# A recommender's forward pass on one core: token rows summed in fours, one comparison a step, one transposed feature buffer, and evictions a step later

## The chip, the cores and the metric

The kernel runs on one core of a Trainium2 chip. The metric is device time in microseconds of one execution, and lower is better. A core has five engines with queues of their own: TensorE (PE, with its weight loads as PEld), VectorE (DVE), ScalarE (ACT), GpSimd (POOL) and SyncE (SP). An engine works through its queue in order. Data comes from HBM by DMA into SBUF, and TensorE writes its results to PSUM.

## The reference

There are 16,384 samples. Each has 32 word indices into a table of 50,000 x 300, three lists of 20 indices into small tables (1000, 5000 and 10000 rows of 64), and four single indices into tables of 100, 50, 20 and 1000 rows of 64. Each small table has a second table of width 1, the "wide" one.

```python
tok = word_emb[token_idx].mean(axis=1)                  # 300 wide
e1 = emb_mh1[mh1_idx].mean(axis=1)                      # e1, e2, e3: 64 wide each
...
o1 = emb_oh1[oh1_idx]                                   # o1 to o4: 64 wide each
...
emb = jnp.concatenate([tok, e1, e2, e3, o1, o2, o3, o4], axis=1)   # 748 wide
wide = (wide_mh1[mh1_idx].sum(axis=(1, 2)) + ... + wide_oh4[oh4_idx][:, 0])
h = relu(emb @ W1 + b1); h = relu(h @ W2 + b2); h = relu(h @ W3 + b3)   # 1024, 512, 256
return sigmoid(h @ Wd + bd + wide)
```

## The kernel before

**Tiles and steps.** The samples are worked through in 128 tiles of 128. A tile takes 11 steps (`STEPS`); a step handles six of the 64 pairs of samples in a tile (`ONEHOT`), and the last step four. The main loop writes all engines' instructions out step by step under a manual schedule, so the order in each engine's queue is the order in which the loop emits them. After the last tile 16 more steps follow (`WAKE`).

**Small tables.** They aren't gathered. Per step `one_hots` compares each key with a row of numbers (`iota`, kept in the PSUM tile `own`) and so makes one-hot rows: `row1` (index modulo 128) and `slice1` (index divided by 128, counted through all 138 slices of all small tables), each with an instruction of its own (L326). ACT scales the upper half of `row1` (L333), so that two samples share one column. `counts` (L344) multiplies the two on TensorE, and ACT packs the result into `cnt` as bytes (L347): how often each row of each table occurs in each sample. One tile later `small_sums` (L363) multiplies `cnt` by the tables, which stand in SBUF as three bf16 terms (`terms`, made at the start by `convert_tables` at a pace set by `TABLE_PACE`), into one PSUM tile `pg` per pair of tables; DVE adds up the three terms into the features `g` (L369).

**Tokens.** The word rows are gathered from HBM by POOL, one indirect DMA for each of the 32 indices of a tile (L259), 128 rows of 300 numbers each, two DMAs to one buffer of `tok_rows`. There are six such buffers. `add_up` adds the two rows to the running sum `tok_sum`, which is in PSUM, with one addition a row (L241, L243, L247), three pairs behind the gathers in the program (`TOK_LAG`). The gathers and additions are spread evenly over all steps.

**Transposes and MLP.** Two steps after a tile's sums are there, `add_small` and `add_tokens` transpose its features on TensorE (four and three transposes, L405, L408, L424, L425), each into a PSUM tile, and DVE copies them with the factors of the means into `x_small`, `x_tok` and `wide_row` (L409 to L427). Three tiles make a block (the last two tiles are blocks of one). Once a block is complete, `mlp` runs on TensorE (L462, f32, up to 384 columns), cut into pieces that are spread over the steps until the next block should be ready. ACT applies bias and ReLU right behind the last matmul of each output (L471).

In a step the loop emits: the one-hots of the next step, `counts` of this one, the table conversion at the start, transposes, gathers and additions, `small_sums` with the reduction behind each pair, then its share of the MLP. At the end, `early_part` begins the last block's first layer with the chunks that need no tokens.

```python
counts(cnt, hot_now, i)
...
if waiting and step >= waiting[0][0]:
    block = transpose(*waiting.pop(0)[1:])
...
toks.to(n_all * (step + 1) / n_steps)
...
    done = next(sums)
...
    layers.to(mlp_work * layers.size * (step + 1 - begin) / left + ahead)
```

Of the kernel before, what the change touches and what calls it, by code (L numbers as in the profile page):

```python
# [23 lines left out]
TOK_GROUP = 2  # L24
TOK_LAG = 3
TOK_BUFS = 6
WAKE = 16
EARLY = 3
BLOCK = 512
# [10 lines left out]
TABLE_PACE = 1.3  # L40
# [5 lines left out]
SMALL = ("o4", "e1", "e2", "e3", "o1", "o2", "o3")  # L46
WIDE_IN_FRONT = ("mh1", "mh3", "oh2")
G_COLS = 7 * ROW
# [7 lines left out]
def kernel(  # L56
# [27 lines left out]
    tables = {"o4": oh4, "e1": mh1, "e2": mh2, "e3": mh3, "o1": oh1, "o2": oh2, "o3": oh3}  # L84
    slices, n_h = {}, 0
    for f in SMALL:
# [9 lines left out]
    ohp = ctx.enter_context(tc.tile_pool(name="onehot", bufs=2))  # L96
# [3 lines left out]
    xsp = ctx.enter_context(tc.tile_pool(name="x_small", bufs=2))  # L100
    xtp = ctx.enter_context(tc.tile_pool(name="x_tok", bufs=2))
# [7 lines left out]

    chunk_rows = [  # L110
        [(300, 428)],
        [(428, 556)],
        [(556, 684)],
        [(684, 748), (256, 300)],
        [(0, 128)],
        [(128, 256)],
    ]
    chunk_k = [sum(b - a for a, b in rows) for rows in chunk_rows]
    NK = len(chunk_rows)

# [4 lines left out]
    scale = const.tile([P, 3], F32, name="scale")  # L125
# [3 lines left out]

# [4 lines left out]
    tok_sum = own[:, 128 : 128 + TOK_D]  # L134
# [13 lines left out]


# [61 lines left out]

# [9 lines left out]
    def load_weights():  # L221
        for k, rows in enumerate(chunk_rows):
            at = 0
            for a, b in rows:
                nc.sync.dma_start(out=w1_sb[at : at + b - a, k, :], in_=w1[a:b, :])
                at += b - a
        nc.sync.dma_start(out=w2_sb, in_=w2.rearrange("(k p) m -> p k m", p=P))
        nc.sync.dma_start(out=w3_sb, in_=w3.rearrange("(k p) m -> p k m", p=P))
        for sb, dram in ((wd_sb, wd), (b1_sb, b1), (b2_sb, b2), (b3_sb, b3), (bd_sb, bd)):
            nc.sync.dma_start(out=sb, in_=dram)  # L230

    n_groups = N_TOK // TOK_GROUP
    n_all = B // P * n_groups + TOK_LAG
    sums_of = {}
    token_indices = {}

    def add_up(t, q, rows):

        a, b = rows[:, 0:TOK_D], rows[:, TOK_D : 2 * TOK_D]
        if q == 0:  # L240
            nc.vector.tensor_add(tok_sum, a, b)  # L241
        else:
            nc.vector.tensor_add(tok_sum, tok_sum, a)  # L243
            to = tok_sum
            if q == n_groups - 1:
                to = sums_of[t] = gp.tile([P, TOK_D], F32, name="g_tok")
            nc.vector.tensor_add(to, tok_sum, b)  # L247

    def tokens():

        under_way = []
        for n in range(n_all):
            if n < n_all - TOK_LAG:
                t, q = divmod(n, n_groups)
                it = token_indices[t // NSUB][:, t % NSUB, :].bitcast(U32)
                rows = tokp.tile([P, TOK_GROUP * TOK_D], F32, name="tok_rows")
                for r in range(TOK_GROUP):
                    j = q * TOK_GROUP + r
                    nc.gpsimd.indirect_dma_start(  # L259
                        out=rows[:, r * TOK_D : (r + 1) * TOK_D],  # L260
                        out_offset=None,
                        in_=word,
                        in_offset=bass.IndirectOffsetOnAxis(ap=it[:, j : j + 1], axis=0),
                    )
                under_way.append((t, q, rows))
            if n >= TOK_LAG:
                add_up(*under_way.pop(0))
            yield 1

    def load_indices(blk):  # L270
# [7 lines left out]
        ix = keyp.tile([P, NSUB // 2, 2, N_SMALL], I32, name="ix")  # L278
        for s in range(NSUB):
            nc.sync.dma_start(  # L280
                out=ix[(s % 2) * HALF : (s % 2 + 1) * HALF, s // 2],
# [7 lines left out]
    def lookup_keys(ix):  # L289

        pairs = NSUB // 2
        low = keyp.tile([P, pairs, 2, N_SMALL], I32, name="low", tag="low")
        nc.vector.tensor_single_scalar(low, ix, P - 1, op=ALU.bitwise_and)
        nc.vector.tensor_single_scalar(ix, ix, 7, op=ALU.logical_shift_right)
        keys = keyp.tile([P, pairs, 2, 2 * N_SMALL], BF16, name="keys", tag="keys")
        for r in range(pairs):
            view = keys[:, r].rearrange("p w (f c) -> p w f c", f=2)
            nc.vector.tensor_copy(view[:, 0], low[:, r])
            nc.vector.tensor_add(view[:, 1], ix[:, r], first)
        return keys  # L300

    def key_columns(keys):


        pairs = NSUB // 2
        pk = ps_h.tile([P, pairs, 2, P], BF16, name="pk", tag="ph")
        for r in range(pairs):
            for w in range(2):
                nc.tensor.transpose(pk[:, r, w, :], keys[:, r, w, :], ident_bf)
        sc = scp.tile([P, pairs, 2, 2, HALF, 2], BF16, name="sc")  # L310
        n = pairs * 2 * P
        nc.vector.tensor_copy(
            sc.rearrange("p r w t b d -> p (r w t b) d"),
            pk.rearrange("p r w b -> p (r w b)").unsqueeze(2).to_broadcast([P, n, 2]),
        )
        return sc

    def one_hots(sc, s, i):
# [3 lines left out]
        row1 = ohp.tile([P, ONEHOT, P], BF16, name="row1")  # L322
        slice1 = ohp.tile([P, ONEHOT, n_h], BF16, name="slice1")
        for w, (one, n) in enumerate(((row1, P), (slice1, n_h))):
            shape = [P, rows, n // 2, 2]
            nc.vector.tensor_tensor(  # L326
                one[:, 0:rows, :].rearrange("p i (n d) -> p i n d", d=2),
                iota[:, 0:n].rearrange("p (n d) -> p n d", d=2).unsqueeze(1).to_broadcast(shape),
                sc[:, s // 2, w, s % 2, b : b + rows, :].unsqueeze(2).to_broadcast(shape),
                ALU.is_equal,  # L330
            )
        upper = row1[HALF:P, 0:rows, :]
        nc.scalar.activation(upper, upper, AF.Copy, scale=UPPER)  # L333
        return row1, slice1

    def counts(cnt, hot, i):
# [5 lines left out]
        for k in range(rows):  # L342
            at = k % n * n_h
            nc.tensor.matmul(  # L344
                pc[:, k // n, at : at + n_h], hot[0][:, k, :], hot[1][:, k, :], start=True, stop=True
# [7 lines left out]
    def small_sums(g, cnt):  # L353
# [3 lines left out]
        for i in (0, 2, 4, 6):  # L357
            pair = SMALL[i : i + 2]
            pg = ps_g.tile([P, 2, 3 * ROW], F32, name="pg")
            for j, f in enumerate(pair):  # L360
                h0, h1 = slices[f]
                for h in range(h0, h1):
# [3 lines left out]
                    yield 1  # L366
            at = i * ROW
            n = len(pair)
            nc.vector.tensor_reduce(  # L369
                g[:, at : at + n * ROW].rearrange("p (f d) -> p f d", f=n),  # L370
                pg[:, 0:n, :].rearrange("p f (c d) -> p f d c", c=3),
                AX.X,
                ALU.add,
            )
            yield None

    def wide_term(g):
# [4 lines left out]
            g[:, EMB : EMB + 6 * ROW].rearrange("p (c d) -> p c d", d=2 * ROW)[:, :, 0:2],  # L382
# [3 lines left out]
        nc.vector.tensor_add(g[:, EMB : EMB + 1], wide, g[:, G_COLS - 1 : G_COLS])  # L386

    class Block:
# [3 lines left out]
        def __init__(self, first, n):  # L392
            self.first, self.n, self.missing = first, n * P, 2 * n
            self.small = xsp.tile([P, 4, N], F32, name="x_small")
            self.wide = wp.tile([1, N], F32, name="wide_row")
            self.tok = None

        def columns(self, t):
            return slice((t - self.first) * P, (t - self.first + 1) * P)

        def add_small(self, t, g):

            at = self.columns(t)
            pt = ps_h.tile([P, 4, P], F32, name="pt", tag="ph")
            nc.tensor.transpose(pt[:, 3, :], g[:, 0:P], ident)  # L405
            for k in range(3):
                c = (1 + 2 * k) * ROW + 1
                nc.tensor.transpose(pt[:, k, :], g[:, c : c + P], ident)  # L408
            nc.vector.tensor_tensor(  # L409
                self.small[:, 0:3, at], pt[:, 0:3, :], scale.unsqueeze(2).to_broadcast([P, 3, P]), ALU.mult  # L410
            )
            nc.vector.tensor_copy(self.small[0:EMB, 3, at], pt[0:EMB, 3, :])  # L412
            nc.vector.tensor_copy(self.wide[:, at], pt[EMB : EMB + 1, 3, :])  # L413

        def add_tokens(self, t, g):


            if self.tok is None:
                self.tok = xtp.tile([P, 2, N], F32, name="x_tok")
            at = self.columns(t)  # L420
            rest = TOK_D - 2 * P
            pt = ps_h.tile([P, 3, P], F32, name="pt", tag="ph")
            for k in range(2):
                nc.tensor.transpose(pt[:, k, :], g[:, k * P : (k + 1) * P], ident)  # L424
            nc.tensor.transpose(pt[0 : EMB + rest, 2, :], g[:, TOK_D - rest - EMB : TOK_D], ident)  # L425
            nc.vector.tensor_single_scalar(self.tok[:, :, at], pt[:, 0:2, :], 1.0 / N_TOK, op=ALU.mult)  # L426
            nc.vector.tensor_single_scalar(  # L427
                self.small[EMB : EMB + rest, 3, at], pt[EMB : EMB + rest, 2, :], 1.0 / N_TOK, op=ALU.mult
            )

        def chunk(self, k):
            x = self.small[:, k, :] if k < 4 else self.tok[:, k - 4, :]
            return x[: chunk_k[k], 0 : self.n]

    def early_part(block):
# [3 lines left out]
        for pair in range(2):  # L439
            two = ps_c.tile([P, 2, 512], F32, name="pc")  # L440
            for m in range(2):
                part.append(two[:, m, :])
                for k in range(NK - 3):
# [8 lines left out]

    def layer(dst, weights, bias, srcs, n_out, part=None):

# [210 lines left out]
```

## Time and profile before

| what | value |
|---|---|
| median of 10 runs | 5192.75 us (5188.0 to 5193.59) |
| the profiled execution | 5189.72 us, its span from the first to the last instruction 5187.9 us |
| PE, PEld busy | 4843.9 us (93%), 3552.2 us (68%) |
| DVE, ACT busy | 3856.3 us (74%), 2758.4 us (53%) |
| POOL busy | 3876.6 us (75%), 4096 gathers of 946 ns |
| DMA | 652 MB, 126 GB/s on average |
| mean granted TensorE clock | 0.983 |

Busy time is the time in which an engine had an instruction under way, by kind of instruction. It doesn't count the time that a queue spends between two instructions, and the ends of pipelined matmuls are modelled. Idle time is put down to what ended it; "issue" is idle time that ends with nothing that the profile shows. A line such as L259 is a line of the listing above.

### The profile page before, as it was taken

To read this page: it belongs to the slowest core of one execution; us is meant where nothing else is said; L and a number is where in the kernel's file an instruction comes from. 1 tells how busy PE (TensorE), PEld (TensorE's weight loads), DVE (VectorE), ACT (ScalarE), POOL (GpSimd) and SP (SyncE) were. 2 spreads that over 40 slices of the span, in tenths; PEclk is the share of its full clock that TensorE was granted. 3 is DMA by queue.
4 is the path that set the end of the run, shared out by engine and by line. 5 is a ranking of instruction groups with operands and counts; after the bars stand their busy time and mean duration, and the time that the engine had idled before them with its cause. 6 is when DMAs were issued, how large, how long until landed. Compare 5 with 4: busy or idle time off the path is not lost.

```text
span 5187.9 us, 94821 instructions
## 1 busy us (share of the span) xinstructions
PE 4843.9 (93%) x34940; PEld 3552.2 (68%) x34940; DVE 3856.3 (74%) x8481; ACT 2758.4 (53%) x3538; POOL 3876.6 (75%) x4103
## 2 busy tenths in 40 slices
PE   7899999999999999999999999999999999999999
PEld 4676676767667766666776667666666666676667
DVE  7777777777777777777777777777777777777773
ACT  6555555555555555555555555555555555555552
POOL 7777777777777777777777777777777777777774
PEclk9999999999999999999999999999999999999999
DMA  7444444444444444444444444444444444444442
GB/s 197 124 126 126 124 127 126 124 125 126 126 124 126 126 126 124 127 126 124 125 126 126 124 126 126 125 124 128 125 123 126 125 126 124 125 126 126 124 124 72
DMA packets 252899, 652.00 MB, mean 126 GB/s; under 512 B 119035, under 2 KB 119591, under 8 KB 252435
## 3 DMA queue, kind: packets, MB, share of 16 engines
q0 software_dynamic: 196608, 629.41, 44.2%
q1 hardware_dynamic: 55827, 16.53, 1.4%
q8 instruction: 276, 4.52, 0.3%
q14 instruction: 188, 1.54, 0.1%
HBM read 645.59 MB, written 0.07 MB: 124 GB/s over the span
## 4 chain that ended last, share of the span: by engine, by line
PE 30%; DMA 24%; DVE 17%; issue 17%; POOL 11%; ACT 1%; DVEq 0%; SPq 0%; POOLq 0%; ACTq 0%
DMA tok_rows<-in_word_emb_dram,it 23%; PE ph L462 17%; POOL tok_rows L259 11%; PE pg L363 9%; DVE own L247 6%; DVE own L243 3%; DVE slice L326 3%; PE pc L344 3%; DVE row L326 2%; PE po L487 1%; DVE g L369 1%; DVE wide_row L413 0%; DVE x_small L427 0%; DMA w_sb<-in_W_dram 0%; DVE x_small L412 0%
## 5 line engine op out<-in xcount | busy, mean ns | idle before, releaser
L259 POOL DMA_INDIRECT tok_rows<-in_word_emb_dram,it x4096 | 3875.8, 946 | 1278.3 <-issue 773.4
L333 ACT ACTIVATE row<-row 64x768 bf16<-64x768 bf16 (+1 forms) x1408 | 1155.4, 821 | 1577.3 <-DVE row L326 1556.0
L363 PE MATMUL pg<-terms,cnt 128*128 128x195 bf16 x17664 | 1760.6, 248 | 223.0 <-DVE g L369 221.8
L363 PEld LDWEIGHTS <-cnt 128*128 128x128 fp8e3 x17664 | 1526.4, 98 | 178.2 <-issue 172.1
L347 ACT ACTIVATE cnt<-pc 128x828 uint16<-128x828 f32 (+1 forms) x1408 | 1191.7, 846 | 157.3 <-PE pc L344 123.0
L462 PE MATMUL ph<-h,w_sb 128*128 128x384 f32 (+1 forms) x3520 | 1260.5, 497 | 0.5 <-ACT h L471 0.5
L247 DVE TENSOR_TENSOR own<-own,tok_rows 128x300 f32<-128x300 f32 x1792 | 857.3, 478 | 468.8 <-DMA tok_rows<-in_word_emb_dram,it 425.7
L243 DVE TENSOR_TENSOR own<-own,tok_rows 128x300 f32<-128x300 f32 x1920 | 918.4, 478 | 265.8 <-DMA tok_rows<-in_word_emb_dram,it 209.8
L462 PE MATMUL ph<-x_small,w_sb 128*128 128x384 f32 (+1 forms) x2784 | 1009.8, 486 | 6.1 <-DVE x_small L409 3.3
L344 PEld LDWEIGHTS <-row 128*128 128x128 bf16 x8192 | 599.7, 98 | 591.4 <-issue 284.5
L462 PEld LDWEIGHTS ph<-h,w_sb 128*128 128x128 f32 x3520 | 636.7, 198 | 388.1 <-issue 110.9
L326 DVE TENSOR_TENSOR row<-own,sc 128x768 bf16<-128x768 bf16 (+1 forms) x1408 | 761.7, 541 | 129.1 <-PE pc L344 29.8
L326 DVE TENSOR_TENSOR slice<-own,sc 128x828 bf16<-128x828 bf16 (+1 forms) x1408 | 795.1, 565 | 0.0
L344 PE MATMUL pc<-slice,row 128*128 128x138 bf16 x8192 | 740.9, 225 | 54.7 <-ACT row L333 53.5
L471 ACT ACTIVATE h<-ph,b_sb 128x384 f32<-128x384 f32 (+1 forms) x612 | 350.0, 572 | 624.4 <-PE ph L462 599.8
L462 PEld LDWEIGHTS ph<-x_small,w_sb 128*128 128x128 f32 x2784 | 484.4, 191 | 246.0 <-issue 20.7
L462 PE MATMUL ph<-x_tok,w_sb 128*128 128x384 f32 (+1 forms) x1392 | 530.3, 485 | 0.0
L369 DVE TENSOR_REDUCE g<-pg 128x130 f32<-128x390 f32 (+1 forms) x512 | 258.4, 505 | 101.2 <-PE pg L363 99.9
L462 PEld LDWEIGHTS ph<-x_tok,w_sb 128*128 128x128 f32 x1392 | 242.0, 191 | 112.6 <-issue 5.2
L241 DVE TENSOR_TENSOR own<-tok_rows 128x300 f32<-128x300 f32 x128 | 61.3, 479 | 110.2 <-DMA tok_rows<-in_word_emb_dram,it 109.1
L426 DVE TENSOR_SCALAR x_tok<-pt 128x256 f32<-128x256 f32 x128 | 53.7, 419 | 107.1 <-PE pt L425 106.6
L409 DVE TENSOR_TENSOR x_small<-pt,scale 128x384 f32<-128x384 f32 x128 | 70.2, 548 | 35.8 <-PE pt L408 34.8
(56 smaller groups left out, 873.8 us busy)
## 6 DMA issues: line engine op xcount, KB each, us to landing
tok_rows<-in_word_emb_dram,it POOLq DMA_INDIRECT x4096
ix<-in_idx_dram SPq DMA_DIRECT2D x128, 32.0 KB
w_sb<-in_W_dram SPq DMA_DIRECT2D x6, 512.0 KB
raw<-in_mh_dram SPq DMA_DIRECT2D x4, 682.5 KB
it<-in_idx_dram SPq DMA_DIRECT2D x32, 64.0 KB
w_sb<-in_W_dram SPq DMA_DIRECT2D x1, 2048.0 KB
out_dram<-h SPq DMA_DIRECT2D x42, 1.5 KB
raw<-in_mh_dram SPq DMA_DIRECT2D x2, 227.5 KB
```

What stands on the lines that cost most here:

```text
L243: nc.vector.tensor_add(tok_sum, tok_sum, a)
L247: nc.vector.tensor_add(to, tok_sum, b)
L259: nc.gpsimd.indirect_dma_start(out=rows[:, r * TOK_D : (r + 1) * TOK_D], out_offset=None, in_=word, in_offset=bass.IndirectOffsetOnAxis(ap ...
L326: nc.vector.tensor_tensor(one[:, 0:rows, :].rearrange("p i (n d) -> p i n d", d=2), iota[:, 0:n].rearrange("p (n d) -> p n d", d=2).unsque ...
L333: nc.scalar.activation(upper, upper, AF.Copy, scale=UPPER)
L344: nc.tensor.matmul(pc[:, k // n, at : at + n_h], hot[0][:, k, :], hot[1][:, k, :], start=True, stop=True)
L347: nc.scalar.activation(cnt[:, :, b : b + rows].rearrange("l h (g k) -> l h g k", g=2), pc[:, :, 0 : n * n_h].rearrange("l g (k h) -> l h g ...
L363: nc.tensor.matmul(pg[:, j, :], by_slice[:, h, :], terms[:, h, :], start=(h == h0), stop=(h == h1 - 1))
L369: nc.vector.tensor_reduce(g[:, at : at + n * ROW].rearrange("p (f d) -> p f d", f=n), pg[:, 0:n, :].rearrange("p f (c d) -> p f d c", c=3) ...
L409: nc.vector.tensor_tensor(self.small[:, 0:3, at], pt[:, 0:3, :], scale.unsqueeze(2).to_broadcast([P, 3, P]), ALU.mult)
L462: nc.tensor.matmul(ph[:, 0:n], weights[: src.shape[0], k, m * P : (m + 1) * P], src, start=(k == 0), stop=(k == len(srcs) - 1),)
L471: nc.scalar.activation(dst[:, m, 0:n], ph[:, 0:n], AF.Relu, bias=bias[:, m : m + 1])
```

## The change

- **Tokens.** A buffer of `tok_rows` now has five rows: four gathered ones (`TOK_GROUP = 4`) and, in front, the sum so far. One `tensor_reduce` adds up the five and writes the result into the front row of the next group's buffer, for the last group into the features. There are three such buffers. The gathers are the same and still emitted two at a time, and the reduction of a group follows when it is three pairs behind.
- **One-hots.** Both one-hots of a sample lie side by side in one tile `hot`, and one comparison over 138 columns makes them; there are three such tiles instead of two.
- **Features.** The small sums and the token sum stand in one buffer `g`, with the columns in an order in which six transposes of 128 columns take in everything, the wide term too (column `WIDE_AT`, with a zero row in `W1`). They go into one PSUM tile of two banks, and one `tensor_tensor` with a factor for each chunk copies all into `x`.
- **Evictions.** What reads TensorE's results is emitted later: the reductions of `pg` and the copies of the transposes at the end of the step (`later`, `flush`) or at the end of the next one, ACT's ReLU ahead of the last matmul of the next output or at the next step's start (`pending`, `flush_outputs`). `small_sums` runs by a fixed table of steps, and most of its matmuls come right behind `counts`.
- **Rest.** Indices are loaded and keys prepared for blocks of two tiles instead of four, `TABLE_PACE` is 1.5 for 1.3, and the order of two tables is swapped.

```diff
-TOK_GROUP = 2
+TOK_PAIR = 2
+TOK_GROUP = 4
 TOK_LAG = 3
-TOK_BUFS = 6
+TOK_BUFS = 3
+HOT_BUFS = 3
-BLOCK = 512
+BLOCK = 256
-TABLE_PACE = 1.3
+TABLE_PACE = 1.5
...
-        a, b = rows[:, 0:TOK_D], rows[:, TOK_D : 2 * TOK_D]
-        if q == 0:
-            nc.vector.tensor_add(tok_sum, a, b)
+        begin = 1 if q == 0 else 0
+        if q == N_TOK // TOK_GROUP - 1:
+            to = features(t)[:, TOK_AT:G_COLS]
+            summed.add(t)
         else:
-            nc.vector.tensor_add(tok_sum, tok_sum, a)
-            to = tok_sum
-            if q == n_groups - 1:
-                to = sums_of[t] = gp.tile([P, TOK_D], F32, name="g_tok")
-            nc.vector.tensor_add(to, tok_sum, b)
+            to = after[:, 0, :]
+        nc.vector.tensor_reduce(to, rows[:, begin:, :].rearrange("p r d -> p d r"), AX.X, ALU.add)
...
-        for w, (one, n) in enumerate(((row1, P), (slice1, n_h))):
-            shape = [P, rows, n // 2, 2]
-            nc.vector.tensor_tensor(
...
+        hot = ohp.tile([P, 2 * ONEHOT, n_h], BF16, name="hot")
+        shape = [P, 2 * rows, n_h // 2, 2]
+        nc.vector.tensor_tensor(
+            hot[:, 0 : 2 * rows, :].rearrange("p i (n d) -> p i n d", d=2),
+            iota.rearrange("p (n d) -> p n d", d=2).unsqueeze(1).to_broadcast(shape),
+            sc[:, at : at + rows].rearrange("p b w d -> p (b w) d").unsqueeze(2).to_broadcast(shape),
+            ALU.is_equal,
+        )
...
+        def transpose(self, t, ks):
...
+            for j, k in enumerate(ks):
+                c = chunk_at[k]
+                nc.tensor.transpose(pt[:, j // n, j % n, :], g[:, c : c + P], ident)
+            def evict():
+                nc.vector.tensor_tensor(
+                    self.x[:, ks[0] : ks[-1] + 1, at : at + P].rearrange("p (a c) b -> p a c b", a=banks),
+                    pt,
...
+    early_sums = {1: sizes_of_pairs[0], 9: sizes_of_pairs[2], **{i: large for i in range(3, 8)}}
+    late_sums = {2: large, 10: sizes_of_pairs[3]}
...
+            flush_outputs()
             counts(cnt, hot_now, i)
             tables_on_chip.to(TABLE_PACE * (step - 2))
...
+        if sums:
+            run_sums(sums, early_sums.get(i, 0), step, step)
         if waiting and step >= waiting[0][0]:
...
         if layers:
             layers.to(mlp_work * layers.size * (step + 1 - begin) / left + ahead)
+        if sums:
+            run_sums(sums, late_sums.get(i, 0), step, step + 1)
+        flush(step)
```

## The prediction

> **What bounds the kernel now.** I read the page's first table, then the costliest groups, then what POOL waited for, then the POOL rows of the timeline, and last the busy time by stretches.
>
> From the page, engines and groups (busy, mean of one, idle before):
>
> ```profile
> PE 4843.9 (93%) x34940; PEld 3552.2 (68%) x34940; DVE 3856.3 (74%) x8481; ACT 2758.4 (53%) x3538; POOL 3876.6 (75%) x4103
> ...
> L259 POOL DMA_INDIRECT tok_rows<-in_word_emb_dram,it x4096 | 3875.8, 946 | 1278.3 <-issue 773.4
> ```
>
> PE looks like the bound at 93%, POOL like an engine with a quarter to spare. The timeline (start, duration, row) says otherwise; here are POOL rows from the first 12 us and from 2000 us:
>
> ```profile
> 4.48 0.95 POOL L259 DMA_INDIRECT tok_rows<-in_word_emb_dram,it  x1 [0.30 <-issue]
> 5.74 0.95 POOL L259 DMA_INDIRECT tok_rows<-in_word_emb_dram,it  x1 [0.30 <-issue]
> 6.99 0.95 POOL L259 DMA_INDIRECT tok_rows<-in_word_emb_dram,it  x1 [0.30 <-issue]
> ...
> 2006.08 0.94 POOL L259 DMA_INDIRECT tok_rows<-in_word_emb_dram,it  x1 [0.30 <-issue]
> 2007.32 0.95 POOL L259 DMA_INDIRECT tok_rows<-in_word_emb_dram,it  x1 [0.30 <-DVE own L247]
> ```
>
> A gather takes 0.95 us and the next starts 0.30 us later, whatever releaser is printed, also among the first gathers, which wait for no buffer. Of the 4,095 intervals between gather starts, 4,072 are under 1.30 us, with a mean of 1.250. So the 0.30 us is part of each gather, POOL is full, and its floor is 4096 x 1.250 = 5120 us of the 5187.9 us span. The rest: first gather at 3.08 us; 33 us in which POOL stood; 32.5 us after the last gather's end at 5155.4.
>
> Where POOL stood (stretch, then busy time of PE, PEld, DVE, ACT, POOL):
>
> ```profile
> 60.00:100.00 40.00, 34.44 (x274) 25.38 (x273) 27.32 (x68) 26.91 (x40) 26.28 (x29) 0.96 0.90 274
> 2000.00:2040.00 40.00, 37.35 (x265) 27.53 (x264) 29.33 (x64) 21.17 (x28) 30.26 (x33) 0.96 0.45 124
> ...
> 5060.00:5090.00 30.00, 30.00 (x145) 19.11 (x144) 14.07 (x33) 10.47 (x16) 22.69 (x25) 1.00 0.46 123
> 5090.00:5120.00 30.00, 30.00 (x147) 19.87 (x146) 7.80 (x17) 3.38 (x6) 16.24 (x18) 1.00 0.34 93
> 5120.00:5150.00 30.00, 29.66 (x216) 24.12 (x214) 9.98 (x24) 5.29 (x12) 10.87 (x12) 1.00 0.20 56
> ```
>
> In 40 us, 30.25 us of POOL (32 gathers of 0.946) is a full queue. The middle is full while PE has 2.65 us to spare: POOL sets the pace. At 60 to 100 us four gathers (about 5 us) are missing, while PE still converts the tables. From 5060 us PE is full and POOL is not: the MLP of the last three-tile block and of the two single tiles is left, and PE sets the end.
>
> So the span is: the end of the gathers of tile 125, about 5 us in which PE was late for it, and 125.7 us of PE's end work. The timeline has these points: tile 125's last gather ends at 5051.4, its sum `g_tok` at 5054.05, its transposes start only at 5058.40 and its MLP at 5062.20.
>
> **The change part by part.**
>
> *Token sums, on DVE.* Out: 31 additions a tile at 478 ns (L241, L243, L247), 14.8 us. In: 8 reductions, seven of 5 x 300 elements and one of 4 x 300. The page's other reduction, L369, takes 556 ns for 390 elements and 351 ns for 195: 1.05 ns an element and 0.146 us fixed. That gives 7 x 1.72 + 1.41 = 13.5 us a tile, 1.3 us less. L369 reads PSUM and the new one SBUF with a long stride; the only reduction from SBUF (L380, 6 elements, 148 ns) has the same fixed part. Worst, at twice the time an element, it is 25.7 us a tile; DVE (30.1 us a tile before) would then be at 39 of POOL's 40 us, and the first rival below would be there. [...]
>
> [...]
>
> *One comparison a step, on DVE.* Out: 554 + 578 ns. In: one of 1656 elements. From the short forms (512 elements 414 ns, 768 in 554) the slope is 0.55 ns: 0.58 + 828 x 0.55 = 1.03 us, 0.1 us less, 1.1 us a tile. ACT's scaling of `upper` starts 0.5 us later in the step; a third one-hot buffer and the step of lead hide it. Without that cover it would be 0.5 us of PE a step, 700 us in all; but the tile is made a step (3.6 us) before `counts` reads it.
>
> *Transposes and evictions.* Out: seven transposes and five copies a tile (548 + 272 + 285 + 419 + 294 = 1.82 us of DVE). In: six transposes and one copy of 768 elements: (548 - 419)/128 = 1.01 ns an element, so 548 + 384 x 1.01 = 0.94 us. About 0.1 us of PE and 0.9 us of DVE a tile.
>
> *Evictions a step later.* PE stood 221.8 us for `pg` behind L369 and 53.5 us for `row`. With the next pair of sums put behind the eviction most of that goes. In the middle it buys nothing: what is late next is the token row, and PE stands for the one-hots behind DVE, which stands for the gather.
>
> *POOL.* The same 4096 gathers of the same shape in the same order. The buffers still hold 12 rows, but in threes of four. Before, a pair is freed by its second addition; its slot is wanted 12 gathers (15.0 us) after the pair's own first gather. Landing comes about 2.0 us after a gather's end (gather 5052.95 to 5053.90, DVE row released by it 5055.92), so DVE may be 15.0 - 2.2 - 2.0 - 0.5 = 10.3 us late before POOL stands. After: 15.0 - 4.7 - 2.0 - 1.7 = 6.6 us. In the trace of before DVE ran at most 3.4 us behind the landing for nine pairs in ten. Holding the rows' release times of the trace against the shorter term, four groups between 120 and 5060 us would have had under 1 us left and one none; that is 0 to 2 us. At the start, where PE's table work makes everything late, the deficit is 2.3 us more than before; the quicker table pace (1.5 for 1.3) brings the work together and may add 2, less waiting may take off as much or all of the 5 us. I take +3, ends -5 and +10.
>
> Whether the new reductions slow descriptor making: the gather's length lies between 0.940 and 0.957 us from the 1st to the 99th percentile beside every kind of DVE work, so I take nothing; 5 ns a gather either way would be 20 us. [...]
>
> *SP.* 64 index loads instead of 32, each half as long, issued at a block's first step for the block one later, some 80 us ahead of use: nothing. What is queued behind them is the output, 1.5 KB a block.
>
> *The end.* Tile 125's last gather ends 3 us later: 5054.4. Landing 2.0, reduction 1.7, six transposes about 0.9 (four take 0.6 at 5155.5), copy 0.94, three hand-overs 0.4: MLP at 5060.3, against 5062.2, if PE is no longer late; -1.9. PE then has more left: 10 sums at 0.087 us and one group of counts, +1.3. Behind the last token row DVE has about 2.5 reductions (4.3 us) where it ran 5.6 us of additions, and PE stood 1.3 us for `g_tok`: -1.5.
>
> **The sum.** 5187.9 - 1.9 + 1.3 - 1.5 = 5185.8 us of span; the profiled execution's own time is 1.8 above its span: 5187.6. It lies 3.0 under the median of the runs (5192.75), so for the median 5190.6 us. This kernel's measurement can tell about 0.2% (10 us) from no change.
>
> **The rivals.**
>
> *POOL stands at every group (slower).* One release for four rows, 6.6 us of room for 10.3. It decides once DVE is over 6.6 us behind the landing in most tiles; the new waits for PE at each step's end (`flush`) could do it, since the reductions queue behind them. For: POOL's lost time is never won back. Against: 90% of pairs are under 3.4 us, and DVE loses 3.3 us of work a tile. At 0.1 to 0.5 us a tile it is 13 to 64 us: around 5215.
>
> *PE was the pacer after all (faster).* Then the 222 + 54 us come back and the time falls below 5120 + 3. Against: full POOL in every middle stretch. What can really be gained is the 5 us at the start, PE's 4.4 us of lateness at tile 125 and up to 7 us of idle in its end work: 5177.
>
> *Nothing is changed in effect:* the main case, within 10 us, since the floor of gathers and PE's end work are both untouched.
>
> **How the numbers follow.** Main case 0.62. POOL standing, or a slower gather, or DVE as the bound: 0.23. Faster by over 10 us needs nearly every small gain at once: 0.15. The range 5176 to 5212 reaches to the faster rival's end and into the slower one; some 2 in 10 stay outside, mostly above.
>
> **What would show it.** Right: the gather's interval stays 1.250 us, POOL at 30.25 us in 40 us stretches, PE with more idle time than 344 us, DVE near 3430 us, the reduction at 1.7 us, MLP of tiles 123 to 125 at about 5060. Wrong: POOL rows with over 0.3 us idle behind the reduction's line all through the middle, another interval, or a reduction of over 2.5 us.

## The result, and the profile after

The changed kernel takes 5309.74 us (median of 8 runs, 5296.42 to 5317.61) against 5192.63 us for the kernel before in the same series: 1.0225 times the time, 95% interval 1.0216 to 1.0234. It is slower by 117 us, where 5190.6 us was predicted and 5212 us was the upper end of the range.

The profiled execution took 5312.93 us, its span 5311.2 us. The engines and the two costliest groups on its page (busy, mean of one, idle before):

```profile
PE 4858.4 (91%) x34812; PEld 3556.8 (67%) x34812; DVE 4542.2 (86%) x3718; ACT 2724.1 (51%) x3538; POOL 3884.4 (73%) x4103
...
L280 POOL DMA_INDIRECT tok_rows<-in_word_emb_dram,it x4096 | 3883.5, 948 | 1393.0 <-issue 1137.9
L265 DVE TENSOR_REDUCE tok_rows<-tok_rows 128x300 f32<-128x1500 f32 (+1 forms) x896 | 2479.2, 2767 | 32.6 <-DMA tok_rows<-in_word_emb_dram,it 32.2
```

DVE has 686 us more of work, not some 426 us less as predicted. The same line with its shapes kept apart, beside the new comparison:

```profile
L265 DVE TENSOR_REDUCE tok_rows<-tok_rows 128x300 f32<-128x1500 f32 x768 | 2195.7, 2859 | 25.8 <-DMA tok_rows<-in_word_emb_dram,it 25.4
L346 DVE TENSOR_TENSOR hot<-own,sc 128x1656 bf16<-128x1656 bf16 x1280 | 1284.7, 1015 | 2.5 <-PE pc L364 1.8 <-issue 0.5
...
L265 DVE TENSOR_REDUCE tok_rows<-tok_rows 128x300 f32<-128x1200 f32 x128 | 283.6, 2215 | 6.8 <-DMA tok_rows<-in_word_emb_dram,it 6.8
```

A reduction of five rows takes 2.86 us, not 1.72. The waits (waiting line, releaser: total, times, longest) say what that does:

```profile
DVE g L389 <- PE pg L399: 435.0, 343, 13.5
...
POOL tok_rows L280 <- DVE tok_rows L265: 163.3, 111, 20.0
DVE h L531 <- PE po L526: 110.1, 39, 23.7
DVE sc L333 <- PE pc L329: 92.5, 51, 7.1
...
DVE x L441 <- PE pc L437: 65.4, 33, 18.2
...
DVE tok_rows L265 <- DMA tok_rows<-in_word_emb_dram,it: 32.2, 35, 3.0
...
DVE g L265 <- DMA tok_rows<-in_word_emb_dram,it: 4.2, 4, 2.5
```

The same waits of the kernel before:

```profile
DVE own L247 <- DMA tok_rows<-in_word_emb_dram,it: 425.7, 728, 3.0
...
DVE own L243 <- DMA tok_rows<-in_word_emb_dram,it: 209.8, 304, 2.6
...
DVE own L241 <- DMA tok_rows<-in_word_emb_dram,it: 109.1, 95, 3.2
...
DVE g L369 <- PE pg L363: 99.9, 67, 5.7
...
DVE g_tok L247 <- DMA tok_rows<-in_word_emb_dram,it: 34.1, 54, 1.6
```

Before, DVE waited 779 us for gathered rows (the sum of L241, L243 and L247), 6 us a tile: that wait was its reserve. After, it waits 36 us for them (32.2 and 4.2), and 710 us for PE (329 us before), mostly for `pg`, `po` and the transposes of keys and features. DVE is busy or waiting for PE nearly all the time, so the rows wait for DVE, and the buffers with them. The timeline shows one such stand (start, duration, row, idle before):

```profile
3204.48 2.86 DVE L265 TENSOR_REDUCE tok_rows<-tok_rows 128x300 f32<-128x1500 f32 x1
...
3211.60 0.55 DVE L531 TENSOR_TENSOR h<-po,x 1x384 f32<-1x384 f32 x1 [4.26 <-PE po L526]
3212.07 0.54 DVE L389 TENSOR_REDUCE g<-pg 128x130 f32<-128x390 f32 x1
...
3215.26 2.83 DVE L265 TENSOR_REDUCE tok_rows<-tok_rows 128x300 f32<-128x1500 f32 x1
3218.02 1.00 DVE L346 TENSOR_TENSOR hot<-own,sc 128x1656 bf16<-128x1656 bf16 x1
3218.36 0.94 POOL L280 DMA_INDIRECT tok_rows<-in_word_emb_dram,it  x1 [3.58 <-DVE tok_rows L265]
3218.95 2.84 DVE L265 TENSOR_REDUCE tok_rows<-tok_rows 128x300 f32<-128x1500 f32 x1
```

DVE waits 4.26 us for `po` at L531; behind that stand an eviction, the transposes' copy, two comparisons and the reduction. POOL stands 3.58 us before its next gather where 0.30 is usual, and reductions follow with one comparison between them. Stretches (busy PE, PEld, DVE, ACT, POOL):

```profile
60.00:100.00 40.00, 30.56 (x241) 22.04 (x239) 26.79 (x24) 25.21 (x40) 19.94 (x22) 0.95 0.79 248
2000.00:2040.00 40.00, 36.29 (x261) 26.87 (x261) 35.65 (x29) 20.64 (x27) 30.30 (x32) 1.00 0.46 126
...
3200.00:3240.00 40.00, 37.39 (x268) 26.64 (x267) 32.97 (x26) 21.12 (x28) 27.82 (x30) 0.98 0.42 115
...
5210.00:5240.00 30.00, 30.00 (x150) 20.10 (x149) 6.19 (x3) 2.91 (x5) 10.13 (x11) 1.00 0.23 62
```

POOL is full in some stretches of the middle (30.30 of 40 us) and 2.4 us short in others; PE has gained idle time it has no use for. From 5180 us PE sets the end again.

By the starts of the gathers (an interval of 1.250 us is none lost), the 123 us that the span grew by lie here; the first gather starts 0.3 us earlier:

| | before | after | difference |
|---|---|---|---|
| lost in gathers 1 to 100 | 5.7 | 17.8 | 12.1 |
| stands (intervals over 1.3 us), gathers 100 to 4032 | 2.5 (16 of them) | 89.3 (89) | 86.8 |
| other intervals there (mean over the run 1.2501, 1.2529) | 0.5 | 11.4 | 10.9 |
| tile 125's last gather's end to its MLP's start | 10.8 | 14.5 | 3.7 |
| from there to the end | 125.7 | 135.6 | 9.9 |

### The profile page after: what moved, and what is told of

Same layout as the page of the kernel before. It is cut to its first block, busy times and chain, and to the rows that moved or that the text cites. A ratio compares the mean times of both kernels' runs of the same rounds, so it can differ in the third digit from the quotient of the medians.

```text
span 5311.2 us, 85279 instructions
## 1 busy us (share of the span) xinstructions
PE 4858.4 (91%) x34812; PEld 3556.8 (67%) x34812; DVE 4542.2 (86%) x3718; ACT 2724.1 (51%) x3538; POOL 3884.4 (73%) x4103
## 4 chain that ended last, share of the span: by engine, by line
PE 43%; POOL 22%; issue 16%; DVE 14%; DMA 5%; ACT 0%; DVEq 0%; POOLq 0%; ACTq 0%
PE ph L495 23%; POOL tok_rows L280 22%; PE pg L399 14%; DVE tok_rows L265 7%; DMA tok_rows<-in_word_emb_dram,it 5%; PE pc L364 4%; DVE hot L346 3%; DVE g L389 2%; DVE g L265 1%; DVE x L441 1%; PE po L526 1%; PE pc L437 1%; DVEq L265 0%; DVE h L531 0%; ACT hot L353 0%
## 5 line engine op out<-in xcount | busy, mean ns | idle before, releaser
L265 DVE TENSOR_REDUCE tok_rows<-tok_rows 128x300 f32<-128x1500 f32 (+1 forms) x896 | 2479.2, 2767 | 32.6 <-DMA tok_rows<-in_word_emb_dram,it 32.2
L353 ACT ACTIVATE hot<-hot 64x768 bf16<-64x768 bf16 (+1 forms) x1408 | 1155.7, 821 | 1830.3 <-DVE hot L346 1820.0
L495 PE MATMUL ph<-x,w_sb 128*128 128x384 f32 (+3 forms) x4176 | 1528.7, 500 | 56.8 <-DVE x L441 56.8
L346 DVE TENSOR_TENSOR hot<-own,sc 128x1656 bf16<-128x1656 bf16 (+1 forms) x1408 | 1375.3, 989 | 2.5 <-PE pc L364 1.8
L495 PEld LDWEIGHTS ph<-x,w_sb 128*128 128x128 f32 (+1 forms) x4176 | 744.1, 196 | 649.6 <-issue 271.7
L364 PEld LDWEIGHTS <-hot 128*128 128x128 bf16 x8192 | 602.1, 98 | 538.3 <-issue 328.7
L364 PE MATMUL pc<-hot 128*128 128x138 bf16 x8192 | 738.6, 226 | 32.8 <-ACT hot L353 26.0
L265 DVE TENSOR_REDUCE g<-tok_rows 128x300 f32<-128x1500 f32 x128 | 366.4, 2863 | 4.3 <-DMA tok_rows<-in_word_emb_dram,it 4.2
L441 DVE TENSOR_TENSOR x<-pc,scale 128x768 f32<-128x768 f32 x127 | 121.0, 953 | 66.0 <-PE pc L437 65.4
L531 DVE TENSOR_TENSOR h<-po,x 1x384 f32<-1x384 f32 (+1 forms) x44 | 23.4, 533 | 110.1 <-PE po L526 110.1
L437 PE MATMUL pc<-ident,g 128*128 128x128 f32 x762 | 104.0, 273 | 0.9 <-ACT cnt L367 0.9
```

The lines of the kernel that those rows point to most:

```text
L265: nc.vector.tensor_reduce(to, rows[:, begin:, :].rearrange("p r d -> p d r"), AX.X, ALU.add)
L346: nc.vector.tensor_tensor(hot[:, 0 : 2 * rows, :].rearrange("p i (n d) -> p i n d", d=2), iota.rearrange("p (n d) -> p n d", d=2).unsqueez ...
L364: nc.tensor.matmul(pc[:, k // n, at : at + n_h], hot[:, 2 * k, 0:P], hot[:, 2 * k + 1, :], start=True, stop=True)
L437: nc.tensor.transpose(pt[:, j // n, j % n, :], g[:, c : c + P], ident)
L441: nc.vector.tensor_tensor(self.x[:, ks[0] : ks[-1] + 1, at : at + P].rearrange("p (a c) b -> p a c b", a=banks), pt, scale[:, ks[0] : ks[- ...
L495: nc.tensor.matmul(ph[:, 0:n], weights[: src.shape[0], k, m * P : (m + 1) * P], src, start=(k == 0), stop=(k == len(srcs) - 1),)
```

## The experiments

Three theories were set against each other (theories 1 to 3 of the expectations). T1: the reduction is slow because it reads elements 1200 B apart, DVE can't catch up after its waits for PE, and POOL stands. T2: three buffers of four rows, freed by one instruction each, leave POOL no slack, whatever the reduction takes. T3: the evictions at the step's end make DVE wait for PE.

**First four runs.** They fell on a chip on which the kernel before itself took 7211.02 us, at a granted TensorE clock of 0.87. In the four profiles taken there (clock 0.84 to 0.85) PE stood 1116 to 1158 us for nothing that the profile shows, and POOL 2534 to 2781 us behind DVE, which itself waited 1598 to 2303 us for PE. So only DVE's durations carry over from there, not the times.

`tokens_undone` is the changed kernel with the token sums as before: six buffers of two rows, an addition a row into PSUM, the last one into `g`.

> The changed kernel with only the token sums put back: six buffers of two rows, one addition a row into the running sum in PSUM. Theory 1 (the reduction reads far-apart rows at 1.9 ns an element, 2.86 us where 1.72 was forecast, so DVE is 35.5 us busy of 40 a tile and can't catch up after its waits for PE): DVE near 28 us a tile, POOL stands as little as in the kernel before, 5175 to 5195 us. Theory 2 (three buffers of four rows, freed by one instruction, leave POOL too little room): the same, 5175 to 5195 us. Theory 3 (the evictions at the step's end make DVE wait for PE): POOL still stands, 5250 us or more.

7530.6 us, 1.0433 times the kernel before there (1.0415 to 1.0452); additions 478 ns.

`adds_of_four` keeps the changed kernel's three buffers of four rows, and sums each group by additions:

```diff
-        nc.vector.tensor_reduce(to, rows[:, begin:, :].rearrange("p r d -> p d r"), AX.X, ALU.add)
+        parts = [rows[:, r, :] for r in range(1, 1 + TOK_GROUP)]
...
+        for k, part in enumerate(parts):
...
+            nc.vector.tensor_add(to, tok_sum, part)
```

> The changed kernel with its three buffers of four rows, all four added when the reduction stood there, but by four additions of 478 ns into PSUM instead of one reduction. Theory 1: within 10 us of the run with the token sums put back, since DVE has 1.9 us a group instead of 2.86. Theory 2: the release is as coarse as in the changed kernel, so it stays above 5270 us. Theory 3: 5250 us or more.

7744.62 us, 1.0737 (1.0721 to 1.0753).

`neighbours` sums five neighbouring elements of the same buffer instead of one of each row (other numbers are added; instructions, buffers and waits stay):

```diff
-        nc.vector.tensor_reduce(to, rows[:, begin:, :].rearrange("p r d -> p d r"), AX.X, ALU.add)
+        nc.vector.tensor_reduce(to, rows[:, begin:, :].rearrange("p r d -> p (r d)").rearrange("p (d r) -> p d r", d=TOK_D), AX.X, ALU.add)
```

> The changed kernel, its reduction reading the same 1500 elements as 300 runs of five neighbours instead of five rows 1200 bytes apart (so other elements are summed: the token features are not those of the reference). If the distance makes the reduction slow: 1.7 us each, and by theory 1 5180 to 5215 us; by theories 2 and 3 5270 us or more in spite of it. If it is slow because its source is SBUF or the result is long: 2.86 us and 5310 us.

7577.17 us, 1.0517 (1.0494 to 1.054). The duration answers: 1.704 us for 1500 elements from the same buffer. The distance makes the difference to 2.86 for sums of five; for fewer terms see below.

`rows_1280_apart` puts the rows 320 numbers apart, in case the distance of 1200 B was a bad one:

> The changed kernel with rows 1280 bytes apart in the buffer instead of 1200, all else the same. If it is the particular distance (a clash of banks) that makes the reduction slow, its time moves clearly from 2.86 us, up or down. If any large distance costs the same, it stays at 2.86 us and the kernel at 5300 to 5320 us.

2.746 us for 1500 elements, 2.235 for 1200 (7765.47 us in one run): hardly better.

**The first and third again,** where the kernel before took 5192.66 us.

> The same kernel as tokens_undone (the changed kernel with only the token sums put back), once more, since the first run was on a chip on which the kernel before itself took 7211 us and PE stood for its own instructions. Where the kernel before takes 5192 us: theory 1 (the reduction's 2.86 us) and theory 2 (coarse release) 5175 to 5195 us with DVE near 28 us a tile; theory 3 (evictions at the step's end) 5250 us or more.

5197.64 us, 1.0011 (1.0001 to 1.002). That is some 3 us above the range expected. All else of the change, evictions included, costs 5 us: T3 falls as the main cause. It is not nothing, though: DVE waits 4.7 us a tile for PE here, against 2.6 before. Between gathers 100 and 4032 POOL lost 4.0 us.

> The same kernel as neighbours (the reduction reads 300 runs of five neighbours instead of five rows 1200 bytes apart; other elements are summed, so the token features are not those of the reference), once more on another chip. If the distance makes the reduction slow: about 1.7 us each, and by theory 1 5180 to 5215 us; by theories 2 and 3 5270 us or more in spite of it. If SBUF as the source or the length makes it slow: 2.86 us and 5310 us.

5208.63 us, 1.0032 (1.0019 to 1.0044); stands in the middle 3.1 us. The group of its reductions:

```profile
L265 DVE TENSOR_REDUCE tok_rows<-tok_rows 128x300 f32<-128x1500 f32 x768 | 1313.1, 1710 | 566.4 <-DMA tok_rows<-in_word_emb_dram,it 564.6 <-DVE hot L346 0.2
```

DVE waits for rows again, and 101 of the 117 us are gone with the same buffers and the same order of instructions. That speaks for T1 and against T2.

**Is it DVE's time, or something else about far-apart reads?** `neighbours_filled` gives the time back as plain work:

```diff
+        nc.vector.tensor_reduce(
+            own[:, 128:320], rows[:, begin:, :].rearrange("p r d -> p (r d)")[:, 0:960].rearrange("p (d r) -> p d r", r=5), AX.X, ALU.add
+        )
```

> The kernel of neighbours_2 (the reduction reads 1,500 neighbouring elements, 1.706 us) with a second reduction of 960 neighbouring elements behind each, whose result nothing reads. 0.146 us and 960 x 1.05 ns make 1.15 us for it, so that both together are 2.86 us, what one reduction over far-apart rows takes. If DVE's time alone is at fault (first theory: 8 x 2.86 us a tile leave DVE 35.5 of 40 us, so that it does not catch up after a wait for PE), the time is again about 5310 us (5290 to 5330), with POOL standing some 90 us behind the reduction's line between gathers 100 and 4032. If there is something else about reading far-apart rows (say that it holds up the gathers' writes), the time stays near neighbours_2, 5205 to 5225 us. The interval of two gathers tells the same in small: 1.2529 us beside the far-apart reads, 1.2500 beside neighbours; it should be 1.250 here if the distance makes it, 1.253 if DVE's being busy does.

5336.8 us, 1.0283 (1.0266 to 1.03), with 123 us of stands in the middle. The two reductions of a group:

```profile
L265 DVE TENSOR_REDUCE tok_rows<-tok_rows 128x300 f32<-128x1500 f32 x768 | 1309.6, 1705 | 14.8 <-DMA tok_rows<-in_word_emb_dram,it 14.4
...
L266 DVE TENSOR_REDUCE own<-tok_rows 128x192 f32<-128x960 f32 x1024 | 1178.7, 1151 | 0.0
```

DVE in the middle was at 35.2 of 40 us as in the changed kernel (35.1; both from 2000 to 2400 us). DVE's time alone brings the loss back, without rows read far apart. It brings 27 us too much, and 7 above the expected range. The filler also follows the groups of four, so that all reductions together take 2885 us against 2846 in the changed kernel; that would account for the excess, but no run separates it. The gathers' interval was 1.2501 us.

> The changed kernel with its three buffers of four rows, but each group of four rows summed by four additions into PSUM (478 ns each) where the reduction stood: 1.91 us a group, 15.3 us a tile, with the same coarse release of the buffers. First theory (the reduction's duration): POOL stands no longer in the middle, 5197 to 5212 us. Second theory (three buffers freed four rows at a time give POOL no slack against DVE's waits for PE): 5270 to 5310 us, with 70 us or more of stands between gathers 100 and 4032. What it takes above tokens_undone_2 (5197.6 us, six buffers of two rows) is the price of the coarse release, 0 to 12 us by neighbours_2.

5203.71 us, 1.0024 (1.0015 to 1.0034), 6.5 us of stands in the middle. T2 falls as a cause by itself: against `tokens_undone_2` the coarse release costs about 6 us. No run joined the long reductions with six buffers, or with the evictions of before, so what these two add to the loss once DVE is short of time is open.

`half_filled` has the same filler with 400 elements in place of 960:

> The kernel of neighbours_filled with 400 elements in the second reduction where it had 960: 0.146 us and 400 x 1.05 ns make 0.57 us each, so DVE is at some 27.2 + 8 x 0.57 = 31.7 of 40 us in the middle, between neighbours_2 (27.2, 5208.6 us) and neighbours_filled (35.2, 5336.8 us). If POOL's stands come from DVE's time running out behind its waits for PE, they set in at a point and don't grow by the microsecond: a slack of 8.3 us a tile is still above the single waits (2 to 5 us) that DVE has to make good, so 5208 to 5225 us with under 15 us of stands in the middle. If every microsecond of DVE's time counts alike, the time lies on the line between the two, 5208.6 + 4.5/8 x 128.2 = some 5281 us.

5214.5 us, 1.0044 (1.0029 to 1.0059), 7.0 us of stands in the middle. The waits for gathered rows and for PE, first of `half_filled`, then of `neighbours_filled`:

```profile
DVE g L392 <- PE pg L402: 502.0, 367, 14.8
DVE tok_rows L265 <- DMA tok_rows<-in_word_emb_dram,it: 256.5, 245, 3.3
```

```profile
DVE g L392 <- PE pg L402: 410.1, 341, 13.7
...
DVE tok_rows L265 <- DMA tok_rows<-in_word_emb_dram,it: 20.8, 23, 2.6
```

At 31.4 of 40 us DVE still waits for rows, and POOL is hardly held; 3.8 us a tile more, and the wait for rows is used up and POOL stands. The loss sets in somewhere between; it does not grow by the microsecond (the straight line gave 5281 us).

**What makes the reduction slow?** `reads_at_distances` puts reductions that nothing reads into the changed kernel, amid the gathers and again after the last of them:

> The changed kernel with reductions that nothing reads put in twice, once in mid-run (step 60 of 128 tiles' steps, gathers under way) and once at the very end, when no gather runs: 1,500 float32 elements of a weight, five to a sum, the five at distances of 1, 2, 4, 12, 60 and 300 elements, then 2, 3, 4 and 8 rows at 300 and 5 rows at 512, then copies of 300 neighbouring and of 300 elements at distance 12. If it is the distance within SBUF that makes the reduction slow, the durations grow from about 1.7 us at distance 1 to 2.86 us at 300, and the mid-run ones equal those at the end within 0.05 us. If the gathers' writes beside it make it slow, those at the end are near 1.7 us at any distance and only the mid-run ones are long. By rows: 300 elements a row at 1.9 ns make 0.57 us for each further row. The time itself is 20 to 40 us above 5310 and is not what is asked.

(5358.43 us in one run.) For 300 sums of five, by single instructions of the trace, in us amid the gathers and after them: distance 1: 1.710, 1.700; 2: 1.724, 1.724; 4: 2.828, 2.821; 12: 2.734, 2.734; 60: 2.858, 2.858; 300: 2.817, 2.817. So it is not the traffic of the gathers. Rows at distance 300, of the same kernel:

```profile
L611 DVE TENSOR_REDUCE own<-w_sb 128x300 f32<-128x2400 f32 x2 | 8.9, 4442 | 0.1
L611 DVE TENSOR_REDUCE own<-w_sb 128x300 f32<-128x1500 f32 x2 | 5.4, 2691 | 0.1
L611 DVE TENSOR_REDUCE own<-w_sb 128x300 f32<-128x1200 f32 x2 | 4.4, 2192 | 0.1
L611 DVE TENSOR_REDUCE own<-w_sb 128x300 f32<-128x900 f32 x2 | 2.4, 1194 | 0.1
L611 DVE TENSOR_REDUCE own<-w_sb 128x300 f32<-128x600 f32 x2 | 1.6, 794 | 0.1
```

(The 1500 here are five rows at distance 512.) Sums of two and three take no more than 1.33 ns an element even 1200 B apart; the fourth row adds 1.00 us, the third 0.40. The expectation of 0.57 us for every further row missed that step.

> The changed kernel with reductions that nothing reads put in twice, in mid-run and at the very end: 300 sums of 2, 3, 4 and 5 float32 elements in SBUF, the elements of a sum 1, 2, 3 and 4 apart; then 60 sums of 3, 4 and 5 at distance 60 from SBUF, the same from PSUM, and from PSUM at distance 1. The last series had 0.79 us for 2 rows at distance 300, 1.19 for 3, 2.19 for 4, 2.82 for 5, 4.44 for 8: 1.1 to 1.2 ns an element to three terms, 1.7 to 1.9 from four on. First theory: the number of terms and a distance of 16 B or more make it together, in SBUF and PSUM alike; then 60 sums of 3 at distance 60 take some 0.35 us in both, of 5 some 0.65 (0.45 at distance 1). Rival: PSUM has no such step, and the row that the prediction took its price from (L369, sums of three from PSUM) was cheap because of the memory: then 5 at distance 60 from PSUM take 0.45 us. The place of the step between distance 2 (1.72 us) and 4 (2.83 us) is asked by distance 3.

Of the 300 sums from SBUF, us by terms and distance:

| terms | 1 apart | 2 apart | 3 apart | 4 apart |
|---|---|---|---|---|
| 3 | 1.10 | 1.10 | 1.10 | 1.17 |
| 4 | 1.41 | 1.41 | 1.41 | 2.28 |
| 5 | 1.72 | 1.72 | 2.11 | 2.82 |

Sixty sums of five, four and three, from PSUM (`own`, distances 60 and 1 together) and from SBUF (`w_sb`, distance 60), groups of `sums_by_terms`:

```profile
L606 DVE TENSOR_REDUCE own<-own 128x60 f32<-128x300 f32 x4 | 1.9, 478 | 0.1
L606 DVE TENSOR_REDUCE own<-own 128x60 f32<-128x240 f32 x4 | 1.7, 416 | 0.1
L606 DVE TENSOR_REDUCE own<-own 128x60 f32<-128x180 f32 x4 | 1.4, 353 | 0.1
L606 DVE TENSOR_REDUCE own<-w_sb 128x60 f32<-128x300 f32 x2 | 1.4, 699 | 0.1
L606 DVE TENSOR_REDUCE own<-w_sb 128x60 f32<-128x240 f32 x2 | 1.1, 568 | 0.1
...
L606 DVE TENSOR_REDUCE own<-w_sb 128x60 f32<-128x180 f32 x2 | 0.7, 368 | 0.1
```

From PSUM the distance costs nothing (478 ns at 60 and at 1); from SBUF five far-apart terms cost 699 ns, three 368. Both theories of that run were half right: it takes SBUF, and more than three far-apart terms to a sum. The step comes between distances 2 and 4 (1.72 and 2.82 us for sums of five, 2.11 at 3). Sums of three hardly have it (1.17 and 1.19 us at distances 4 and 300, 0.07 and 0.10 above distance 1). What makes the step, no run showed. A plain copy of 300 numbers is slower too at distance 12 (678 ns, 474 as neighbours).

**The end.** `before_last_five` is the kernel before with one number changed, `LAST_TILES = 5` for 2, to try whether PE's work at the end can be moved forward:

> The kernel before, with the last five tiles in blocks of a tile of their own where it was the last two (the tiles 123 to 125 no longer wait for each other). If the end from 5060 us on is set by PE, as the prediction read it (125.7 us of matmuls behind tile 125's transposes, 86 of them of the block of three), the MLPs of 123 and 124 move ahead of tile 125's last gather, into time in which PE waits for gathers, and the end comes when POOL's last gather allows: 5155.4 plus the single tile behind it, some 5160 to 5172 us. If the end is POOL's alone, with PE's work beside it, nothing moves: 5188 to 5196 us. A block of one tile costs PE more than a third of a block of three, so a loss of up to 10 us is the other side.

5191.7 us, 0.9999 (0.9989 to 1.0008): no change. Its stretches from 4940 and 5100 us:

```profile
4940.00:4980.00 40.00, 40.00 (x208) 26.37 (x209) 18.55 (x41) 14.49 (x20) 25.93 (x28) 1.00 0.41 111
4980.00:5020.00 40.00, 40.00 (x227) 26.77 (x226) 15.12 (x33) 13.73 (x19) 12.98 (x14) 1.00 0.18 49
...
5100.00:5140.00 40.00, 38.71 (x375) 37.53 (x374) 20.59 (x49) 9.19 (x22) 30.25 (x33) 1.00 0.46 124
```

By the time alone this could as well be the other reading, that the end is POOL's; the stretches show where the gain went. The block of tiles 120 to 122 now had to be done within one tile's time: PE is full from 4940 to 5020 us and POOL stands there (31 us in the middle) instead of at the end (none lost in the last 64 gathers, 24.1 before). PE's work was there to be moved, but no idle time to move it into; the 5160 to 5172 us expected were wrong.

## Why the prediction was wrong

**The failed step is the first term, the token sums.** The 1.72 us for a reduction of five rows measured 2.86 us, and that of four 2.22 us: 7 x 2.86 + 2.22 = 22.2 us a tile, not 13.5. The price came from L369, sums of three out of PSUM; the new reduction is sums of five out of SBUF. Either difference alone would have left the row a good one (300 sums of three from SBUF at most 0.10 us above neighbours, 60 sums of five from PSUM 478 ns at distances 60 and 1 alike); together they add two thirds. The text saw memory and stride, and named "twice the time an element" as the worst (1.9 ns were measured); it then took the near end. None of the float32 rows that it had to go by (L369 from PSUM at 1.05 ns an element, the additions of 300 numbers in 478 ns) summed far-apart numbers out of SBUF.

**The bound was put at the wrong place.** By the text DVE comes to 39 of 40 us at the worst rate, and that counts its work alone. POOL stood already at 35.1 of 40 us. What was not counted is DVE's waits for PE: an engine that works in order has its own work and its waits for engines other than the one it keeps up with. Work and waits for PE in us a tile, from each run's page and waits, against POOL's 40: 30.1 + 2.6 before, 27.0 + 7.7 in `neighbours_2` and 31.1 + 6.8 in `half_filled`, all three with under 10 us of stands in the middle; 35.5 + 5.5 in the changed kernel and 35.5 + 5.3 in `neighbours_filled`, with 89 and 123 us. The range, too, ended at 5212 us, though the text's own worst case led into the first rival.

**The rival that came** is the first, "POOL stands at every group", with a chance of 0.23. The end of its chain was right (late reductions, late buffers, POOL's lost time), its start and its size were not. It made the waits for PE from `flush` decide; `neighbours_2` has the same `flush`, 7.7 us a tile of waits for PE and 3.1 us of stands, so the reduction's length decided. The stands in the middle grew by 87 us where it had 13 to 64, priced with reductions of 1.72 us. It stood at 89 of some 980 groups, in bursts, not at every one.

**The smaller terms.** With the reduction at 1.71 us (`neighbours_2`) the whole change takes 5208.6 us, within the range but 18 above the forecast. By its profile (5204.51 us) the span is 14.8 us longer than before: 7.7 until tile 125's last gather (predicted +3; the start alone lost 7.4), 3.1 from there to the MLP, 4.0 behind. The step "if PE is no longer late" failed: the reduction of tile 125 ends at 5063.24, and its transposes run at 5069.45, behind sums, counts and older MLP work in PE's queue. 13.9 us from gather to MLP stand against 5.9 predicted, and 129.8 us behind it against 125.5. "Most of that goes", of PE's 222 us behind the eviction of `pg`, failed as well: it is 270 us in `neighbours_2`, 289 in `tokens_undone_2` and 332 in the changed kernel.

**What was right.** POOL is the pacer and the 0.30 us belong to the gather: `tokens_undone_2`, `neighbours_2` and `adds_of_four_2` have intervals of 1.250 us and come within 16 us of before. DVE's other costs were met: the comparison 1.015 us (1.03), the copy of the transposes 0.953 us (0.94). That PE sets the end was seen again in the changed kernel (30.00 of 30 us from 5210). Taking nothing for slower gathers is neither confirmed nor refuted. The changed kernel's interval was 1.2529 us, 12 us in all, but `reads_at_distances` has the same far-apart reductions and 1.2502, and `neighbours` has near ones and 1.2530. So the distance doesn't make it, and what does is open.

## What to carry to other kernels

Take the price of a new instruction from a row with the same memory, the same distance between consecutive reads and the same number of terms to a sum; where there is none, the worst bound must go through to the end time. For float32 rows of 300 in SBUF, four additions (4 x 478 ns) took less here than one reduction of five (2.86 us), and one addition of two rows (0.48 us) less than a reduction of two (0.79 us). Whether an engine can take more work is read from its waits for the pacer (here DVE's for gathered rows): 779 us before, 292 us with half the filler, 36 us when the pacer stood.

## What the runs showed of the hardware

- In `sums_by_terms`, 300 float32 sums from SBUF took 1.17 us with three terms and 2.28 us with four, the terms 16 B apart (neighbours: 1.10 and 1.41). From PSUM, 60 sums of three, four and five took 353, 416 and 478 ns at distances 60 and 1 alike.
- A copy of 300 float32 numbers from SBUF took 474 ns as neighbours and 678 ns at distance 12 (`reads_at_distances`).
- The interval of the gathers in the changed kernel's profile was 1.2529 us instead of 1.2501, 12 us in all. `reads_at_distances` has the same reductions and 1.2502, `neighbours` has near ones and 1.2530; the cause is open.
- The kernel before took 39% longer on another chip (7211.02 us), at a granted TensorE clock of 0.87 for 0.98. Four variants profiled there had PE standing 1116 to 1158 us for nothing that the profile names.
